# The forget gate's convolution of two recurrences by three VectorE taps on one projection, in place of four shifted TensorE products

## The chip, the cores and the metric

The kernel runs on one core of a Trainium2 chip. A core has TensorE (PE, matmuls; PEld is its weight load), VectorE (DVE), ScalarE (ACT), GpSimd (POOL) and SyncE (SP, which only issues transfers here). The metric is the device time of one execution in microseconds (us), lower is better. A profiled execution has a span, which the profile's rows divide, and a slightly longer time that counts what lies around it.

## The reference

The input x holds 4 sequences of 512 tokens with 128 channels, fp32. One block of a model is computed, each part on a layer norm of x and added to x:

1. a power attention with 16 heads of 8 channels and learned decay,
2. a mixture of experts: 8 experts, the best 2 for each token, hidden width 352,
3. a gated linear recurrence (HGRN),
4. the mixture of experts again.

The edited part is the third:

```python
i_raw = causal_depthwise_conv(x @ Wi, conv_i)      # 4 taps along time, per channel
f_raw = causal_depthwise_conv(x @ Wf, conv_f)
g_raw = x @ Wg
f = sigmoid(f_raw)
i = silu(i_raw) * (1 - f)
h_t = f_t * h_{t-1} + i_t                          # scan over the 512 tokens
o = h * rsqrt(mean(h*h) + eps) * g_norm_weight * silu(g_raw)
out = o @ Wo
```

A causal depthwise convolution with 4 taps is `sum over k of xp[:, k:k+T] * w[:, k]`, with 3 zeros ahead of the sequence.

## The kernel before

A planner (class Plan, lines 46 to 198) orders all work. Each piece of work is an `op` with an estimated cost on each engine that may do it, a priority, the tiles it reads and writes, and tiles it holds. The planner takes one op after the other, picks the engine and the order by these estimates, and gives out tiles from pools as they come free: "k2", 16 tiles of 128 x 512; "pad", 4 tiles with 3 zero columns ahead; "b1", single banks of PSUM. The instructions are issued on each engine in that order, so another cost or another engine for one op can move everything planned after it. Where the planner sees a gap on TensorE it puts filler matmuls (line 195).

Sequences are worked in two halves, q = 0 (sequences 0 and 1) and q = 1 (sequences 2 and 3); gen = 1 is the first mixture of experts and gen = 2 the second; stage (gen, q) is one of them for one half. The order is: attention for all, and for each stage

- `route(gen, q, i)` (line 865), for sequence i of the half: layer norm (lines 548 to 562) and transposition (L570), scores on TensorE (L875), the two best experts on VectorE (L899 to L920, exponential on ACT at L901), the token's scaled copies xk (L941 on ACT or L943 on VectorE), ranks by a small product (L927, L929), places (L952 to L998: i = 1 needs those of i = 0; L985 is the first that reads the ranks), and 8 scatters by GpSimd (L1004) that put rows of xk into the table xg; an i = 1 also computes `of` (to L1030), the offsets of the experts' weights for each block of 128 rows.
- `experts(gen, q)` (line 1042): 20 blocks. SP reads the expert's offset from `of` (L1089) and loads the block xb from xg (L1056) and the weights (L1099). TensorE transposes (L1068) and multiplies (L1106, L1126), ACT and VectorE do the gate (L1119, L1122), one of them copies the result (L1132), and GpSimd scatters it into the table yg (L1139).
- `combine` (line 1150): SP loads two tiles from yg for each sequence (L1158), VectorE (or GpSimd at the end) adds them to x (L1167).
- after gen 1, `hgrn` (line 1174) for each sequence, in priority beside the rest of the experts' work of the other half.

So a recurrence's result goes through the layer norm to the router of stage (2, q), whose VectorE work sets GpSimd's scatters and SP's loads.

In `hgrn(b)`, `xnT` is the normalized sequence with the channels on partitions, and hw holds Wi, Wf, Wg, Wo. The steps are

- L1180: `pi`, one product Wi by xnT (two passes on the chip for fp32).
- L1183: `pf`, four products of `wfk[k]` (Wf scaled by tap k, built once, L526 to L538) with xnT shifted by k, added up in one bank of PSUM.
- L1186: `pg`, one product with Wg.
- L1189 and L1193: the convolution of i: `acc = pi * tap 3` by ACT or VectorE, then three VectorE taps that read `pi` from PSUM shifted by one, two and three tokens and add into `acc`.
- L1196: `ft = tanh(0.5 * pf)` on ACT; L1198: silu of `acc`; L1202 and L1203: gate and input; L1205: the scan on VectorE; L1207, L1209, L1210: silu of `pg`, squares, gated output.
- L1215 and L1219: mean square by a product with ones, and the product with Wo; L1223 and L1225: the inverse root, the power on GpSimd; L1228: VectorE adds the result to x.

Of the kernel before, what the change touches and what calls it, by code (L numbers as in the profile page):

```python
# [11 lines left out]
AF = mybir.ActivationFunctionType  # L12
ALU = mybir.AluOpType
# [32 lines left out]
class Plan:  # L46
# [14 lines left out]
    def op(self, engs, fn, r=(), w=(), pri=0.0, late=None, after=(), hold=(), size=0.0,  # L61
           table=None):
        vals = list(hold)
        for v in hold:
            v.users += 1
        o = Op(dict(engs), fn, vals, pri, late, size, table)
        o.preds.update(after)
        for how, items in ((0, r), (1, w)):
            for it in items:
                v, part = it if isinstance(it, tuple) else (it, None)  # L70
                if v not in vals:
                    vals.append(v)
                    v.users += 1
                hit = v.parts if part is None else [p for p in (part, None) if p in v.parts]
                for p in hit:
                    o.preds.update(v.parts[p][0])
                    if how:
                        o.preds.update(v.parts[p][1])
        for how, items in ((0, r), (1, w)):
            for it in items:  # L80
                v, part = it if isinstance(it, tuple) else (it, None)
                if how:
                    if part is None:
                        v.parts = {}
                    v.parts[part] = ([o], [])
                else:
                    if part is None and v.parts:
                        for p in v.parts:
                            v.parts[p][1].append(o)
                    else:  # L90
                        v.parts.setdefault(part, ([], []))[1].append(o)
        o.preds.discard(o)
        self.ops.append(o)
        return o
# [147 lines left out]
def block_pass(  # L242
# [20 lines left out]
    nc = tc.nc  # L263
    B, T, C = x.shape
# [6 lines left out]
    CK = conv_i.shape[1]  # L271
    PAD = CK - 1
# [58 lines left out]
    op = plan.op  # L331

    def fixed(shape, nm, dt=FP):
        return Val(None, tile_of(shape, nm, dt))

    def new(kind):
        return Val(kind)

    def ve(n, ps=False):
        return 0.12 + n * (0.00098 if ps else 0.0009)  # L340

    def act(n):
        return 0.215 + n * 0.00071
# [4 lines left out]
    def either(n):  # L348
        return {"DVE": ve(n, True), "ACT": act(n)}
# [4 lines left out]
    def pe(n, passes=2):  # L354
        return passes * (0.03 + n * 0.0008)
# [17 lines left out]
    wfk = fixed([P, CK, C], "wfk")  # L373
# [4 lines left out]
    hw = fixed([P, 4, C], "hw")  # L378
    cw = fixed([P, 2, CK], "cw")
# [11 lines left out]
    slots_v = [Val(None, t) for t in vt + ot + gst + padt + xkt]  # L391
# [6 lines left out]
    def sp(fn, r=(), w=(), pri=0.0, late=2.2, after=(), cost=0.5, size=0.1, q="SP"):  # L398
# [4 lines left out]
       w=[xs[0]], pri=PRE, size=1.3)  # L403
# [4 lines left out]
    for b in range(1, B):  # L408
        sp(lambda e, b=b: e.dma_start(out=xs[b].t, in_=x[b].rearrange("(n p) c -> p n c", p=P)),
           w=[xs[b]], pri=PRE + 2 + b, size=1.3)  # L410

    def pl(fn, r=(), w=(), pri=PRE, n=128):
# [12 lines left out]
       r=[upto], w=[negm], pri=INIT)  # L425
# [5 lines left out]
       r=[ident], w=[hsel], pri=INIT)  # L431
# [12 lines left out]
    for k, t in enumerate(wst):  # L444
# [3 lines left out]
       r=[upto, ident], w=[upto_b], pri=-600.0)  # L448
# [22 lines left out]
    for k in range(14):  # L471
# [6 lines left out]
       r=[wnat, ident], w=[pw], pri=PRE)  # L478
# [695 lines left out]
    def hgrn(b, pri):  # L1174
        xn, xnT = new("k2"), new("pad")
        normed(b, xn, 0, pri)
        turned(xn, 0, xnT, PAD, pri)
        pf, pi, pg = new("b1"), new("b1"), new("b1")
        acc, ft, fg, sg, u, o, o2 = (new("k2") for _ in range(7))
        op({"PE": pe(T)}, lambda e: e.matmul(pi.t, hw.t[:, 0, :], xnT.t[:, PAD:], start=True, stop=True),  # L1180
           r=[(hw, 0), xnT], w=[pi], pri=pri, hold=[acc])
        op({"PE": CK * pe(T)}, lambda e: [
            e.matmul(pf.t, wfk.t[:, k, :], xnT.t[:, k : k + T], start=(k == 0), stop=(k == CK - 1))  # L1183
            for k in range(CK)
        ], r=[wfk, xnT] + slots_v[6:10], w=[pf], pri=pri, hold=[ft])
        op({"PE": pe(T)}, lambda e: e.matmul(pg.t, hw.t[:, 2, :], xnT.t[:, PAD:], start=True, stop=True),  # L1186
           r=[(hw, 2), xnT], w=[pg], pri=pri, hold=[sg])
        op(either(T), lambda e: (
# [2 lines left out]
           r=[pi, cw], w=[acc], pri=pri)  # L1191
        for k in range(PAD - 1, -1, -1):
            op({"DVE": 0.75}, lambda e, k=k: e.scalar_tensor_tensor(  # L1193
                acc.t[:, PAD - k : T], pi.t[:, 0 : T - PAD + k], cw.t[:, 0, k : k + 1], acc.t[:, PAD - k : T],
                ALU.mult, ALU.add), r=[pi, cw, acc], w=[acc], pri=pri)
        op({"ACT": act(T)}, lambda e: e.activation(ft.t, pf.t, AF.Tanh, scale=0.5),  # L1196
           r=[pf], w=[ft], pri=pri, table=("silu", "exp"))
        silus.append(op({"ACT": act(T)}, lambda e: e.activation(u.t, acc.t, AF.Silu),  # L1198
                        r=[acc], w=[u], pri=pri, table=("silu",)))
        op({"ACT": act(T), "DVE": ve(T)}, lambda e: (  # L1200
# [5 lines left out]
           r=[fg, u], w=[o], pri=pri)  # L1206
        silus.append(op({"ACT": act(T)}, lambda e: e.activation(sg.t, pg.t, AF.Silu),  # L1207
                        r=[pg], w=[sg], pri=pri + 1, table=("silu",)))
# [18 lines left out]
        for n in range(NB):  # L1227
# [3 lines left out]
               w=[(xs[b], None) if n == 0 else (xs[b], ("n", n))], pri=pri)  # L1231
# [4 lines left out]
    with tc.manual_schedule():  # L1236
# [15 lines left out]
        for gen in (1, 2):  # L1252
            for q in range(2):
                experts(gen, q, 100.0 * (2 * gen + q))
                for i in range(2):
                    combine(gen, q, i, CH[q] + i, gen == 2)
                    if gen == 1:
                        hgrn(seqs(q)[i], CH[q] + i)
                        route(2, q, i, CH[q] + (1.0 if i == 0 else 5.0))
# [4 lines left out]
        if over is not None:  # L1264
            op({"DVE": 0.2}, lambda e: e.tensor_scalar(over[1], over[0], float(NS), None, ALU.is_gt),
               r=[over_v], w=[over_v], pri=1000.0)
# [45 lines left out]
```

## Time and profile before

| | us |
|---|---|
| median of 3 runs | 535.82 (533.52 to 535.88) |
| profiled execution | 532.88 |
| span of the profiled execution | 530.7 |
| TensorE busy in it | 444.4 (84%) |
| VectorE busy | 301.3 (57%) |
| ScalarE busy | 300.8 (57%) |
| GpSimd busy | 249.1 (47%) |

The profiled execution lies 2.18 us over its own span and 2.9 us below the median. Its page has the busy time of each engine, the span cut in 40 slices of 13.3 us with the busy tenth of each engine and TensorE's granted clock, the chain of work that ended last, and the costliest groups of instructions. In a chain, "issue" is time in which an engine waited for nothing that the profile shows. In the list of waits a line names the waiting group and what released it, the total, the number of times and the longest.

The four recurrences run at 301 to 320 us (sequences 0 and 1, beside the last blocks of stage (1,1)) and at 393 to 415 us (sequences 2 and 3, beside the blocks of stage (2,0)).

### The profile page before, as it was taken

The page shows a single profiled execution, that of the slowest core. Times are in us where ns is not written, and L with a number is a line of the kernel's source. Part 1 is how long each engine was busy: PE and PEld are TensorE (multiplying, and loading weights), DVE is VectorE, ACT ScalarE, POOL GpSimd, SP SyncE. Part 2 cuts the span into 40 slices and gives each one's busy share as a digit, 9 for nine tenths or more (in the row PEclk, how much of TensorE's full clock was granted, in tenths as well). Part 3 has the DMA queues.
Part 4 walks back from the last instruction along what each step waited for, and adds up shares of the span by engine and source line. Part 5 has one row for each costly group of instructions (what it writes and reads, how often), then busy time and mean ns, then how long its engine had stood idle before and what let it go on. Part 6 is the DMA issues. An engine that isn't in the chain of part 4 may idle for free.

```text
span 530.7 us, 12313 instructions
## 1 busy us (share of the span) xinstructions
PE 444.4 (84%) x4319; PEld 346.7 (65%) x4319; DVE 301.3 (57%) x893; ACT 300.8 (57%) x512; POOL 249.1 (47%) x414
## 2 busy tenths in 40 slices
PE   8898999799869996999679999655999967689970
PEld 7554455355536562789579779645977957589960
DVE  7878598459848884675312776820177764013212
ACT  4689998599949994866124455601254643024420
POOL 6344154425362436334755536485063664816540
PEclk9999999699989997899979999857999987879995
DMA  3025100293083011226348814135582423639604
GB/s 94 12 58 143 47 1 17 73 187 50 5 229 95 1 30 40 61 82 182 109 133 265 256 35 131 55 86 150 152 252 56 124 81 98 178 110 312 201 21 124
DMA packets 67943, 57.55 MB, mean 108 GB/s; under 512 B 8576, under 2 KB 65822, under 8 KB 67872
## 3 DMA queue, kind: packets, MB, share of 16 engines
q1 hardware_dynamic: 60096, 46.65, 33.2%
q0 software_dynamic: 4608, 8.44, 4.7%
q10 hardware_dynamic: 3168, 1.57, 1.0%
q8 instruction: 37, 0.61, 0.5%
q14 instruction: 34, 0.28, 0.2%
HBM read 41.68 MB, written 16.00 MB: 109 GB/s over the span
## 4 chain that ended last, share of the span: by engine, by line
PE 53%; DVE 15%; issue 12%; ACT 10%; POOL 3%; DMA 2%; SPq 1%; another core or an unknown queue 1%; POOLq 0%; DVEq 0%; ACTq 0%
PE ps L1106 15%; PE ps L1126 9%; PE ps L719 6%; ACT k L735 4%; POOL yg L1139 3%; PE ps L777 3%; PE ps L1183 3%; PE ps L195 2%; ACT k L730 2%; ACT dec L703 2%; PE ps L773 2%; PE ps L1068 2%; PE ps L694 1%; PE ps L875 1%
## 5 line engine op out<-in xcount | busy, mean ns | idle before, releaser
L1106 PE MATMUL ps<-k,ws 128*128 128x128 f32 x960 | 125.6, 285 | 14.2 <-issue 13.5
L1106 PEld LDWEIGHTS ps<-k,ws 128*128 128x128 f32 x960 | 118.7, 200 | 17.9 <-issue 16.6
L1139 POOL DMA_INDIRECT yg<-y,xb x80 | 80.6, 1008 | 94.3 <-ACT y L1132 64.0
L1122 DVE TENSOR_TENSOR k<-k,ps 128x384 f32<-128x384 f32 x80 | 42.1, 548 | 114.4 <-PE ps L1106 59.8
L735 ACT ACTIVATE k<-k,aeps 128x1024 f32<-128x1024 f32 (+1 forms) x96 | 92.8, 1019 | 3.1 <-DVE k L731 2.8
L1126 PE MATMUL ps<-we,k 128*128 (+1 forms) x480 | 71.6, 296 | 14.8 <-issue 7.8
L1004 POOL DMA_INDIRECT xg<-xk,slt x64 | 62.8, 981 | 37.5 <-DVE slt L998 14.8
L1126 PEld LDWEIGHTS ps<-we,k 128*128 128x128 f32 (+1 forms) x480 | 64.1, 207 | 17.9 <-issue 9.0
L719 PE MATMUL ps<-k,k 32*128 32x384 f32 (+3 forms) x512 | 61.5, 498 | 8.0 <-issue 4.0
L1119 ACT ACTIVATE k<-ps 128x384 f32<-128x384 f32 x77 | 36.6, 489 | 51.5 <-PE ps L1106 32.9
L1132 ACT ACTIVATE y<-ps 128x128 f32<-128x128 f32 x72 | 19.7, 276 | 75.2 <-PE ps L1126 33.2
L751 POOL TENSOR_TENSOR k<-k,dec 128x256 f32<-128x256 f32 x29 | 22.2, 767 | 68.7 <-ACT k L735 45.1
L730 ACT ACTIVATE k<-ps 128x1024 f32<-128x1024 f32 (+1 forms) x49 | 45.8, 959 | 12.4 <-PE ps L719 5.5
L731 DVE TENSOR_SCALAR k<-ps 128x1024 int32<-128x1024 int32 (+1 forms) x47 | 44.2, 953 | 10.8 <-PE ps L719 8.2
L719 PEld LDWEIGHTS ps<-k,k 32*128 32x128 f32 x512 | 30.5, 198 | 24.2 <-issue 9.2
L195 PE MATMUL ps<-ones 128*128 128x128 f32 x232 | 37.1, 302 | 7.7 <-issue 7.7
L777 PE MATMUL ps<-k,vo 128*18 128x128 f32 x768 | 38.6, 280 | 5.0 <-ACT k L735 4.6
L362 ACT COPY k<-ps 128x512 f32<-128x512 f32 (+1 forms) x43 | 24.1, 571 | 29.2 <-PE ps L1068 18.3
L195 PEld LDWEIGHTS ps<-ones 128*128 128x128 f32 x232 | 32.2, 210 | 11.7 <-issue 9.7
L746 POOL TENSOR_TENSOR k<-k,dec 128x256 f32<-128x256 f32 x31 | 24.8, 812 | 27.7 <-ACT k L735 25.9
L703 ACT ACTIVATE dec<-ps 128x1024 f32<-128x1024 f32 x32 | 32.9, 1032 | 6.2 <-PE ps L719 3.7
L777 PEld LDWEIGHTS ps<-k,vo 128*18 128x18 f32 x768 | 21.2, 98 | 20.1 <-ACT k L735 14.6
(193 smaller groups left out, 625.4 us busy)
## 6 DMA issues: line engine op xcount, KB each, us to landing
ws<-in_L_ffn_w_dram SPq DMA_DIRECT2D x160, 176.0 KB
xb<-xg SPq DMA_DIRECT2D x20, 258.0 KB
xg<-zero SPq DMA_DIRECT2D x8, 451.5 KB
k<-yg SPq DMA_DIRECT2D x12, 256.0 KB
xg<-zero SPq DMA_DIRECT2D x4, 387.0 KB
yg<-y,xb POOLq DMA_INDIRECT x80
x<-in_L_attn_a_x_dram SPq DMA_DIRECT2D x4, 256.0 KB
we<-in_L_ffn_w_dram SPq DMA_DIRECT2D x8, 128.0 KB
```

Of the source, the lines that this page charges most:

```text
L195: self.nc.tensor.matmul(self.pairs[i][2][:, h, 0 : self.idle.shape[1]], self.idle, self.idle, start=True, stop=True)
L703: exps.append(op({"ACT": act(2 * T)}, lambda e: e.activation(dec[half].t, pd.t.rearrange("p k t -> p (k t)"), AF.Exp), r=[pd], w=[dec[half ...
L719: e.matmul(sps[hh // 2].t[:, hh % 2, c : c + tn * P], kT.t[r, s * P : (s + 1) * P], qT.t[r, t0 * P : (t0 + tn) * P], start=True, stop=True)
L730: e.activation(view(), sps[pr].t[:, :, 0:n], AF.Abs)
L731: if e is nc.scalar else e.tensor_scalar(view().bitcast(I32), sps[pr].t[:, :, 0:n].bitcast(I32), 0x7FFFFFFF, None, ALU.bitwise_and)
L735: op({"ACT": act(2 * n)}, lambda e, pa=pa: e.activation(pa.t, pa.t, AF.Square, bias=aeps.t), r=[pa, aeps], w=[(pa, "o"), (pa, "d")], pri=p ...
L777: e.matmul(oo.t[rows, (i - 1) * P : i * P], s, p, start=(ev == 0 and (i, j) == (1, 0)), stop=(ev == 1 and j == i - 1), skip_group_check=True)
L1004: d = e.indirect_dma_start(out=xgv.t, out_offset=bass.IndirectOffsetOnAxis(ap=slot.t[:, k * NB + n : k * NB + n + 1], axis=0), in_=xk[k].t ...
L1106: e.matmul(ph.t[:, w, kk * P : (kk + 1) * P], ws.t[:, w * HID + kk * P : w * HID + (kk + 1) * P], xT.t[:, k * P : (k + 1) * P], start=True ...
L1122: op({"DVE": ve(HD, True) + 0.03}, lambda e, ph=ph, sl=sl, hT=hT: e.tensor_tensor(hT.t[:, 0:HD], sl.t[:, 0:HD], ph.t[:, 1, 0:HD], ALU.mult ...
L1126: e.matmul(hp.t[:, 0:C], hT.t[0:fn, kk * P : (kk + 1) * P], wf[0:fn, bass.ds(regs[j] + kk * NE * C, C)], start=(kk == 0), stop=(kk == NF_ ...
L1139: d = e.indirect_dma_start(out=ygv.t, out_offset=bass.IndirectOffsetOnAxis(ap=xb.t[:, k, C : C + 1].bitcast(I32), axis=0), in_=y.t, in_off ...
```

## The change

For the sequences of the first half (`b < B // 2`) the forget gate's projection is one product with the unscaled Wf, and the convolution is done afterwards: tap 3 by a scaling out of PSUM (ACT or VectorE) into a new "k2" tile `cf`, taps 2, 1 and 0 by three VectorE instructions that read `pf` from PSUM, as it is done for `pi`. The tanh reads `cf` in place of `pf`. For the second half `cf` is `pf` and nothing differs. The scaled weights `wfk` are still built, since the second half uses them. The changed op also names Wf, (hw, 1), among what it reads. In the changed file the lines below the edit stand 13 further on.

```diff
-        op({"PE": CK * pe(T)}, lambda e: [
-            e.matmul(pf.t, wfk.t[:, k, :], xnT.t[:, k : k + T], start=(k == 0), stop=(k == CK - 1))
-            for k in range(CK)
-        ], r=[wfk, xnT] + slots_v[6:10], w=[pf], pri=pri, hold=[ft])
+
+        beside = b < B // 2
+        cf = new("k2") if beside else pf
+        op({"PE": (1 if beside else CK) * pe(T)}, lambda e: [
+            e.matmul(pf.t, wfk.t[:, k, :] if not beside else hw.t[:, 1, :], xnT.t[:, k : k + T],
+                     start=(k == 0 or beside), stop=(k == CK - 1))
+            for k in range(PAD if beside else 0, CK)
+        ], r=[wfk, (hw, 1), xnT] + slots_v[6:10], w=[pf], pri=pri, hold=[ft] + [cf] * beside)
+        if beside:
+            op(either(T), lambda e: (
+                e.activation(cf.t, pf.t, AF.Copy, scale=cw.t[:, 1, PAD:CK]) if e is nc.scalar else
+                e.tensor_scalar(cf.t, pf.t, cw.t[:, 1, PAD:CK], None, ALU.mult)),
+               r=[pf, cw], w=[cf], pri=pri)
+            for k in range(PAD - 1, -1, -1):
+                op({"DVE": 0.75}, lambda e, k=k: e.scalar_tensor_tensor(
+                    cf.t[:, PAD - k : T], pf.t[:, 0 : T - PAD + k], cw.t[:, 1, k : k + 1], cf.t[:, PAD - k : T],
+                    ALU.mult, ALU.add), r=[pf, cw, cf], w=[cf], pri=pri)
...
-        op({"ACT": act(T)}, lambda e: e.activation(ft.t, pf.t, AF.Tanh, scale=0.5),
-           r=[pf], w=[ft], pri=pri, table=("silu", "exp"))
+        op({"ACT": act(T)}, lambda e: e.activation(ft.t, cf.t, AF.Tanh, scale=0.5),
+           r=[cf], w=[ft], pri=pri, table=("silu", "exp"))
```

## Prediction

> **What bounds the kernel now.** I read the busy line first, then the slices, the chain that ended last, and the stretch from 300 to 420 us in windows, because the edited lines run there for the first two recurrences.
>
> ```profile
> PE 444.4 (84%) x4319; PEld 346.7 (65%) x4319; DVE 301.3 (57%) x893; ACT 300.8 (57%) x512; POOL 249.1 (47%) x414
> ...
> PE   8898999799869996999679999655999967689970
> ...
> PEclk9999999699989997899979999857999987879995
> ```
>
> TensorE (PE) leads, but not evenly: in slices 26 to 28 (332 to 371 us, 13.3 us each) its row falls to 6, 5, 5 and the granted clock to 0.8, 0.5, 0.7.
>
> ```profile
> 300.00:320.00 20.00, 19.84 (x109) 13.73 (x108) 14.68 (x35) 9.76 (x20) 7.57 (x9) 1.00 0.27 76
> 320.00:340.00 20.00, 18.02 (x163) 17.74 (x163) 15.06 (x73) 14.72 (x29) 10.75 (x19) 1.00 0.32 92
> 340.00:360.00 20.00, 9.43 (x51) 8.71 (x51) 7.31 (x33) 1.83 (x6) 17.11 (x32) 0.66 0.28 80
> 360.00:380.00 20.00, 15.20 (x107) 14.40 (x108) 1.09 (x3) 2.83 (x8) 5.42 (x10) 0.83 0.48 135
> ```
>
> (Busy us of PE, weight load, VectorE (DVE), ScalarE (ACT) and GpSimd (POOL), then the clock.) The edited products run where PE is full, 300 to 320; the hole they must shorten is at 346 to 377. The chain of work says the same:
>
> ```profile
> 302.25 3.43 PE ps L1183 x8
> ...
> 309.21 3.43 PE ps L1183 x8
> ...
> 312.64 0.89 PE ps L1219 x8
> ...
> 346.17 5.75 issue
> 351.92 4.75 PE ps L1106 x24
> ...
> 374.34 2.83 DMA xb<-xg
> ```
>
> Both four-product groups are on the chain, 3.43 us each. What feeds the hole is told by the waits of SP, ACT and POOL there:
>
> ```profile
> SPq L1089 <- DVE of L1030: 16.2, 1, 16.2
> ...
> ACT k L1119 <- remote: 12.5, 1, 12.5
> ...
> POOL xg L1004 <- DVE slt L998: 6.2, 1, 6.2
> ```
>
> SP reads expert numbers (L1089) and loads the blocks xb of stage (2,0) only after VectorE has finished the offsets (L1030, at 347.5); POOL starts its 16 scatters L1004 only when VectorE has the slots (L998, 336.9). So from 302 to 347 a chain leads from recurrence to normalization to router, mostly of VectorE latency. Then comes something I can see but not explain: from 348.4 to 364.2 all queues but POOL step about one instruction per 0.70 us (SP's register moves take 0.02 to 0.04 elsewhere), so ACT idles 12.5 us. It goes with unbroken runs of POOL's indirect transfers: 337.4 to 361.2 here, and 427.1 to 438.4 in the second half, where L985 waits 6.51 us.
>
> **The change part by part.** What moves I take from the two kernels' orders of instructions on each engine. Only the recurrences of sequences 0 and 1 change (302 to 320 us).
>
> Removed: three of four products. L1183 has 8 matmul passes per recurrence in 3.43 us of chain, 0.43 a pass; 6 passes go: 2.57 us, for two recurrences 5.15 us of PE.
>
> Added: one scaling from PSUM, like L1189 (0.678 us, on ACT in the new order), and three taps like L1193 (0.748 us; three dependent ones took 303.01 to 305.33, 2.32). Together 1.36 us of ACT and 4.6 us of VectorE. VectorE is 14.7 of 20 us busy here, so room exists, but the taps stand on the recurrence's own path: tanh (L1196) waited for the fourth product until 305.95; now it waits for the sixth tap.
>
> First recurrence: in the new order both conv's taps alternate. Six taps from 303.0 at about 0.77 end near 307.5 (305.33 before); tanh ends near 308.1 (306.54), the scan near 310.4 (308.85), the gated output L1210 near 311.25 (309.70): 1.55 us later. But its Wo product L1219 started only at 312.48, behind the second recurrence's L1183 (309.04 to 312.48) on PE. That queue is 5.15 us shorter, so L1219 starts at about 311.5, the ones-product L1215 ends near 313.1 (314.2) and x is updated at 316.1 (317.8): 1.6 us earlier, not 5.15. VectorE is what is late next.
>
> Router of sequence 0: L875 (326.05) comes 2.1 us earlier, L904 (330.18) 3.2; then three of L562 and two of L1122 are newly ahead of it on VectorE, and L998 ends 2.05 earlier. In POOL's new order one scatter of stage (1,1), L1139, moved from behind the 16 L1004 to before them, at 1.26 us pitch (337.35 to 338.62 for one): the scatters start about 1.5 us earlier, near 335.9.
>
> Second recurrence and router of sequence 1: the same taps, tanh 1.5 us later against its products, PE earlier by 5.15 less what waits for VectorE; offsets L1030 about 1.1 us earlier (346.4).
>
> Moved besides: on SP the four combine loads L1158 now stand ahead of a pair of weight loads L1099; SP waited 16.2 us right after, so they cost nothing unless that wait ends 4 × 0.7 us earlier. The seven L1089 stay seven (0.47 each). In the last stage one more addition L1167 stands on POOL instead of VectorE; it belongs to the last 17 us, where loads of 2.66 and 6.41 us bound it: between −0.3 and +1.0 us, taken as 0. The pool of 16 tiles holds one more for each of the two recurrences; the new order shows no engine's work displaced by it beyond what I listed: 0, and at most one tap chain, 2.3 us, if a normalization waits for a tile.
>
> From 347 on: the slow stretch is bounded by nothing on show. If it follows POOL's run, it shifts with it: −1.5 us. Then SP's loads and PE's (2,0) blocks start 1.1 to 1.5 us sooner, and the second half (PE full 380 to 420, all four products kept) is the same work.
>
> Sum: profiled execution 532.88 (span 530.7 and 2.18 around it) − 1.5 = 531.4. That execution lies 2.9 us under the median of the runs, 535.82, so in the median's terms 534.3.
>
> A rule that speaks against the change: the Trainium skill, VectorE: DVE Perf Modes, section Rules for kernel authors, advises accepting the slow rate for one operation on a matmul output, but copying it to SBUF if many follow. Here the rows are 748 ns for a tap on PSUM and 683 to 692 for the like-shaped L1203 on SBUF: three taps would gain 0.2 us and the extra copy costs 0.68, so by the row the rule would not pay and the sum keeps the PSUM taps; by the rule, 0.4 us for the two recurrences would be left lying, sum 531.0.
> Another, Perfetto Trace Analysis, section Identifying the Most-Contended Engine, says to optimize the engine of highest occupancy first; followed to the letter PE's 5.15 us would come off in full, 527.7. The waits above, on VectorE's L998 and L1030, make me take 1.5.
>
> **Rivals.**
> 1. Slower: the slow stretch falls on router work. One mechanism, place: POOL's run and the rank and place chain L985 to L1030 of sequence 1 (VectorE, 342 to 347.5). Before, this chain lay 5.8 to 10.2 us into the run and lost 0.7 us. With the scatter L1139 joined at the front, the run starts near 334.6, and the chain (1.1 earlier) lies 7.4 to 11.8 us into it. In the second half the slow stretch caught L985 about 8 us into its run and cost 6.51 us. The point from which it decides: L985 more than about 8 us after the run's first transfer. Price: up to 6.51 − 1.5 = +5.0: 537.9 profiled, 540.8 in the median. The run also holds six L1139 after the scatters, so the slowness may last to about 366 instead of 364.2. For it: the shifts just given. Against: 0.7 us of that chain was already inside without harm.
> 2. Faster: PE's 5.15 us comes through in full, because PE is on the chain from 299 to 334: 530.7. Or the blocks of (1,1) that now go ahead leave less in the slow stretch: SP alone needs 12.3 us after L1030, so the loads could begin near 359 instead of 374, at most −14 us. For it: in the new order all L1106 of (1,1) stand before the last rank product (before, two blocks, 351.9 to 356.7, did not). Against: VectorE's later tanh, and SP's slowness itself.
> 3. Nothing: PE's freed time fills with idle or filler matmuls (L195), the router leaves VectorE when it did: 535.8.
>
> **How the numbers follow.** About 0.5% (2.7 us) is what a measurement can tell from no change. Case A (−1.5, own range 532 to 537): 0.37. Rival 1, in full or in part (537 to 543): 0.34. Rival 2 (524 to 532): 0.25. Rival 3: 0.04. A is the likeliest: 534.3. Faster: rival 2 and 0.05 from A's low edge, 0.30. Same: A's middle, 0.28, and rival 3, 0.32. Slower: rival 1 and 0.04 from A's high edge, 0.38. Range: rival 1's whole price is 540.8, with the slow stretch's 1.8 us extra 542.6; rival 2's full PE gain 530.7, with about a third of the 14 us, 526. So 526 to 542 leaves about 0.2 out.
>
> **What will show it.** The edited product at 2 passes and 0.86 us; three taps at 0.75 and a 0.68 us scaling; tanh of the first recurrence released by VectorE near 307.5; x of sequence 0 at 316.1 instead of 317.8; L998 near 334.9 and the first L1004 near 335.9; SP's wait for the offsets ending near 346.4; first xb of (2,0) landing near 375.7 instead of 377.2; the end at 529.2 of span. It is wrong if ACT's "remote" idle moves from 12.5 us to over 16 or under 8, if L985 of sequence 1 waits several us, or if the second half's 6.51 us wait on L985 changes, which I priced at 0.

## The result and the profile after

| | before | changed |
|---|---|---|
| median, 8 runs each | 535.5 us (530.11 to 537.79) | 540.73 us (537.56 to 543.73) |
| ratio | 1 | 1.0103, 95% interval 1.0066 to 1.0139 |
| span of the profiled execution | 530.7 us | 536.6 us |

The changed kernel is 1.0% slower. A later measurement of the same two, beside three other kernels, gave 1.0152 (1.0094 to 1.0211). The forecast was 534.3 us, 1.5 less than before, which counted as no change; its largest single chance, 0.38, stood on slower. The measured time lies where the slower rival put it (540.8); whether for that rival's reason is taken up below.

The page of the changed kernel begins with this busy line:

```profile
PE 446.7 (83%) x4345; PEld 347.5 (65%) x4345; DVE 302.1 (56%) x897; ACT 303.6 (57%) x518; POOL 250.4 (47%) x415
```

TensorE has twelve passes of 512 columns less, and is busy 2 us longer all the same: the filler matmuls L195 rose from 232 to 270. The stretches around the edit (busy us of TensorE, weight load, VectorE, ScalarE and GpSimd, then the clock):

```profile
300.00:320.00 20.00, 19.09 (x135) 15.77 (x133) 17.64 (x45) 13.88 (x29) 8.27 (x14) 1.00 0.42 118
320.00:340.00 20.00, 17.14 (x155) 16.69 (x154) 16.79 (x73) 13.40 (x27) 12.04 (x17) 1.00 0.22 63
340.00:360.00 20.00, 11.44 (x88) 11.00 (x87) 7.49 (x37) 4.70 (x16) 11.73 (x23) 0.83 0.23 66
360.00:380.00 20.00, 11.42 (x67) 9.90 (x65) 0.00 (x0) 0.00 (x0) 10.20 (x20) 0.74 0.41 109
```

VectorE rose from 14.68 to 17.64 us in the first and from 15.06 to 16.79 in the second; in the last, VectorE and ScalarE did nothing at all for 20 us. What happened between is read from VectorE's timeline of the changed kernel (start, length, engine, line, operation; in brackets the idle time before it and what ended it):

```profile
304.34 1.53 DVE L1206 SCALAR_TENSOR_TENSOR k<-ps,cw,k 128x511 f32<-128x511 f32 x2 [0.80 <-ACT k L1202]
...
307.10 1.52 DVE L1196 SCALAR_TENSOR_TENSOR k<-ps,cw,k 128x510 f32<-128x510 f32 x2
...
310.44 1.23 DVE L1218 TENSOR_TENSOR_SCAN k<-k,k 128x512 f32<-128x512 f32 x1
311.70 0.75 DVE L1223 SCALAR_TENSOR_TENSOR k<-k,gn,k 128x512 f32<-128x512 f32 x1
312.37 0.74 DVE L1206 SCALAR_TENSOR_TENSOR k<-ps,cw,k 128x511 f32<-128x511 f32 x1
...
316.11 1.12 DVE L1241 SCALAR_TENSOR_TENSOR x<-ps,st,x 128x128 f32<-128x128 f32 x4
317.14 0.74 DVE L1196 SCALAR_TENSOR_TENSOR k<-ps,cw,k 128x509 f32<-128x509 f32 x1
...
319.54 1.19 DVE L1218 TENSOR_TENSOR_SCAN k<-k,k 128x512 f32<-128x512 f32 x1
```

The second recurrence's products are there at 310, but its taps begin at 312.37, because the first recurrence's taps and scan hold VectorE, and they end at 317.8, because x of sequence 0 (L1241) is in between. Its scan starts at 319.54. In the kernel before, the same instruction is

```profile
314.55 1.23 DVE L1205 TENSOR_TENSOR_SCAN k<-k,k 128x512 f32<-128x512 f32 x1
```

To leave out that this execution began its first recurrence 1.33 us later, I count from the first projection (301.1 and 302.5). The update of x of sequence 0 then starts at 13.7 us instead of 15.5, 1.9 earlier; that of sequence 1 at 23.5 instead of 19.3, 4.2 later; the scores of sequence 1's router (L875) at 34.2 instead of 27.6, 6.6 later.

In this pair of profiles the lateness goes no further. VectorE works through the router of sequence 0 first, and takes up the choice of experts for sequence 1 (L904 is its first step behind the exponential) at the same time as before, 36.5 us after the first projection in the kernel before and 36.6 in the changed one:

```profile
337.64 0.17 DVE L904 TENSOR_REDUCE sm<-sm 128x4 f32<-128x32 f32 x1
```

```profile
339.06 0.17 DVE L904 TENSOR_REDUCE sm<-sm 128x4 f32<-128x32 f32 x1
```

What is lost comes behind it.

The waits of the changed kernel from 330 to 390 us:

```profile
POOL xg L1004 <- issue: 9.2, 16, 6.4
ACT y L1132 <- remote: 9.1, 1, 9.1
DVE sm L985 <- PE ps L929: 7.4, 1, 7.4
```

and SP's own in that stretch:

```profile
SPq L1089 <- DVE k L1122: 25.3, 1, 25.3
```

Sequence 1's rank product (L929) was caught in the stretch in which ScalarE hardly steps: L985 waited 7.4 us, GpSimd's 16 scatters broke into 8 and 8 with a hole of 6.4, and SP got the offsets at 354.8 instead of 347.7. The first xb of stage (2,0) was issued at 378.4 instead of 374.3. A second profile of each showed the same: 382.0 after, 377.0 before, L985 waiting 7.5 us after and not at all before. There the choice of sequence 1 began later too, at 40.3 us against 36.6, and that of sequence 0 at 30.1 against 29.1; why is not shown. Counted from the first projection, the first xb of (2,0) was issued at 76.0 and 80.9 us in the changed kernel and at 73.2 and 74.9 before.

### The profile page after: what moved, and what is told of

The parts are those of the page before. It is cut to its first block, busy times and chain, and to the rows that moved or that the text cites. A ratio compares the mean times of both kernels' runs of the same rounds, so it can differ in the third digit from the quotient of the medians.

```text
span 536.6 us, 12357 instructions
## 1 busy us (share of the span) xinstructions
PE 446.7 (83%) x4345; PEld 347.5 (65%) x4345; DVE 302.1 (56%) x897; ACT 303.6 (57%) x518; POOL 250.4 (47%) x415
## 2 busy tenths in 40 slices
DMA packets 67943, 57.55 MB, mean 107 GB/s; under 512 B 8576, under 2 KB 65822, under 8 KB 67872
## 4 chain that ended last, share of the span: by engine, by line
PE 43%; DVE 18%; issue 12%; ACT 9%; POOL 7%; another core or an unknown queue 4%; DMA 3%; SPq 3%; POOLq 0%; DVEq 0%; ACTq 0%
PE ps L1106 11%; PE ps L1126 7%; PE ps L719 6%; POOL yg L1139 5%; PE ps L777 3%; ACT k L735 3%; PE ps L773 2%; ACT dec L703 2%; PE ps L1186 2%; PE ps L694 2%; SPq L1099 2%; ACT k L730 1%; DVE gst L466 1%; DVE k L1122 1%
## 5 line engine op out<-in xcount | busy, mean ns | idle before, releaser
L1106 PE MATMUL ps<-k,ws 128*128 128x128 f32 x960 | 123.6, 283 | 13.4 <-ACT y L1132 7.6
L1106 PEld LDWEIGHTS ps<-k,ws 128*128 128x128 f32 x960 | 115.9, 197 | 17.7 <-ACT y L1132 7.7
L1122 DVE TENSOR_TENSOR k<-k,ps 128x384 f32<-128x384 f32 x80 | 42.2, 549 | 116.3 <-PE ps L1106 81.2
L1126 PE MATMUL ps<-we,k 128*128 (+1 forms) x480 | 69.2, 291 | 7.6 <-DVE over L1022 2.9
L1126 PEld LDWEIGHTS ps<-we,k 128*128 128x128 f32 (+1 forms) x480 | 62.6, 203 | 10.8 <-issue 3.7
L719 PE MATMUL ps<-k,k 32*128 32x256 f32 (+3 forms) x512 | 62.5, 512 | 7.0 <-issue 4.0
L195 PE MATMUL ps<-ones 128*128 128x128 f32 x270 | 46.6, 314 | 21.9 <-issue 15.1
L195 PEld LDWEIGHTS ps<-ones 128*128 128x128 f32 x270 | 39.5, 219 | 28.4 <-issue 19.8
L362 ACT COPY k<-ps 128x512 f32<-128x512 f32 (+1 forms) x43 | 24.1, 570 | 47.8 <-PE ps L1068 36.6
L746 POOL TENSOR_TENSOR k<-k,dec 128x256 f32<-128x256 f32 x31 | 25.2, 825 | 27.9 <-ACT k L735 26.1
```

The lines of the kernel that those rows point to most:

```text
L195: self.nc.tensor.matmul(self.pairs[i][2][:, h, 0 : self.idle.shape[1]], self.idle, self.idle, start=True, stop=True)
L719: e.matmul(sps[hh // 2].t[:, hh % 2, c : c + tn * P], kT.t[r, s * P : (s + 1) * P], qT.t[r, t0 * P : (t0 + tn) * P], start=True, stop=True)
L1106: e.matmul(ph.t[:, w, kk * P : (kk + 1) * P], ws.t[:, w * HID + kk * P : w * HID + (kk + 1) * P], xT.t[:, k * P : (k + 1) * P], start=True ...
L1122: op({"DVE": ve(HD, True) + 0.03}, lambda e, ph=ph, sl=sl, hT=hT: e.tensor_tensor(hT.t[:, 0:HD], sl.t[:, 0:HD], ph.t[:, 1, 0:HD], ALU.mult ...
L1126: e.matmul(hp.t[:, 0:C], hT.t[0:fn, kk * P : (kk + 1) * P], wf[0:fn, bass.ds(regs[j] + kk * NE * C, C)], start=(kk == 0), stop=(kk == NF_ ...
```

## The experiments

All ratios are to runs of the kernel before made beside them. "x of sequence 0" and "x of sequence 1" are the starts of their updates and "first xb" is the issue of the first xb of stage (2,0), all in us from the first projection. The kernel before has 15.5, 19.3 and 73.2 or 74.9 in its two profiles, the changed one 13.7, 23.5 and 76.0 or 80.9.

| run | what | stretches | ratio (95%) | x of sequence 0 | x of sequence 1 | first xb |
|---|---|---|---|---|---|---|
| order_only | new order, four products, no taps | yes | 1.0163 (1.0136 to 1.0191) | 18.8 | 27.9 | 82.2 |
| oneprod | one product, no taps, own order | yes | 0.9999 (0.9972 to 1.0026) | 11.5 | 18.8 | 74.7 |
| first_only | taps for sequence 0 | yes | 0.9951 (0.9932 to 0.9970) | 14.8 | 18.6 | 75.9 |
| first_again | the same, later | yes | 1.0040 (1.0006 to 1.0074) | 14.8 | 18.6 | 74.8 |
| second_only | taps for sequence 1 | yes | 1.0006 (0.9983 to 1.0028) | 12.1 | 21.9 | 77.1 |
| work_only | old order, one product, taps | yes | 1.0114 (1.0077 to 1.0150) | 19.4 | 23.4 | 81.1 |
| hold_after | changed, scatters held back | yes | 1.0132 (1.0085 to 1.0179) | 13.7 | 23.5 | 73.8 |
| after_gap_2 | changed, scatters 3.4 us later | yes | 1.0144 (1.0100 to 1.0189) | 13.7 | 23.5 | 77.2 |
| before_late_2 | before, choice of sequence 1 later | yes | 1.0011 (0.9981 to 1.0041) | 15.5 | 19.3 | 72.1 |
| after_gap | changed, scatters 3.4 us later | no | 1.0018 (0.9987 to 1.0048) | 13.6 | 23.4 | 60.4 |
| before_gap | before, scatters 3.4 us later | no | 1.0050 (1.0021 to 1.0079) | 15.4 | 19.2 | 60.8 |
| before_late | before, choice of sequence 1 later | no | 1.0036 (1.0002 to 1.0069) | 15.4 | 19.2 | 60.9 |
| first_gap | taps for sequence 0, scatters later | no | 1.0052 (1.0018 to 1.0085) | 14.7 | 18.5 | 62.3 |
| taps_added | old order, four products, taps | no | 1.0112 (1.0074 to 1.0150) | 20.8 | 24.8 | 67.8 |
| prods_removed | old order, one product, no taps | no | 1.0010 (0.9980 to 1.0041) | 16.3 | 20.0 | 61.1 |

One thing must be known to read them. In the runs marked "no" the kernel before took 484 to 485 us, in all others 534 to 538, and in those six traces there is no stretch with steps of 0.70 us at all. Ratios are only taken within a group.

**First: order, products, or taps?**

order_only (new order of everything, work of before):

```diff
-            e.matmul(pf.t, wfk.t[:, k, :] if not beside else hw.t[:, 1, :], xnT.t[:, k : k + T],
-                     start=(k == 0 or beside), stop=(k == CK - 1))
-            for k in range(PAD if beside else 0, CK)
+            e.matmul(pf.t, wfk.t[:, k, :], xnT.t[:, k : k + T], start=(k == 0), stop=(k == CK - 1))
+            for k in range(CK)
...
-                op({"DVE": 0.75}, lambda e, k=k: e.scalar_tensor_tensor(
...
+                op({"DVE": 0.75}, lambda e: None, r=[pf, cw, cf], w=[cf], pri=pri)
```

> The planner is given the changed ops, so that every other instruction stands in the changed kernel's order, but the forget gate is still made by four products and the scaling and the taps emit nothing; the output is complete. Theory V (VectorE's taps of the second recurrence make the router of sequence 1 late, so that its rank product falls into the stall of GpSimd's first eight scatters): without taps the second recurrence's scan starts near 315.5 instead of 319.5, the wait of L985 is under 1 us, the 16 scatters form one run, and the time is 534 to 537. Rival O (the new order alone costs it, above all the scatter moved ahead of the 16): the wait of 7.4 us stays and the time is 540 to 543.

Measured: 545.72 us, 1.0163, L985 waits 7.6 us, the second scan at 323.3. Theory V's numbers failed here: without taps it was slower still. But this order was planned for a short TensorE queue, and the products push everything in it back (x of sequence 1 at 27.9 us), so the run does not tell what the order costs by itself.

oneprod:

```diff
+        k0 = PAD if b < B // 2 else 0
-        op({"PE": CK * pe(T)}, lambda e: [
+        op({"PE": (CK - k0) * pe(T)}, lambda e: [
...
-            for k in range(CK)
+            for k in range(k0, CK)
```

> One product with the scaled weights of tap 3, no taps on VectorE: the forget gate's three other taps are left out for sequences 0 and 1. It is the change's saving on TensorE without its cost on VectorE. Theory V: the scan of the second recurrence starts 3 to 5 us earlier than in the changed kernel, the wait of L985 is gone, and the time is 529 to 534. Rival P (TensorE's time does not matter here at all): 535 to 536.5. Rival O (order): anything from 535 to 541 with a wait of several us on L985 in spite of the early scan.

Measured: 537.87 against 537.01, 0.9999. Taking 5.15 us of work from the busiest engine, with nothing put in its place, bought nothing. The saving did reach the router: x of sequence 0 came at 11.5 us instead of 15.5 and its slots (L998) at 30.7 instead of 35.8. So GpSimd's run began at 332.4, sequence 1's rank product was caught (L985 waited 8.4 us), as the slower rival had it, and by the first xb (74.7) the gain was gone. With three taps left out the experts chosen can differ, but the transfers moved as much (57.54 MB, 57.55 before).

first_only and second_only (`beside = b == 0` and `beside = b == 1`):

> Only sequence 0 uses the taps, sequence 1 keeps the four products. Theory V: the second recurrence's scan is late by at most 1.5 us, the wait of L985 stays under 2 us, time 534 to 537. If half of the loss comes from each recurrence alone: 538.

> Only sequence 1 uses the taps. Theory V: six taps of the second recurrence on VectorE beside the first one's update of x; the scan of the second is late by 1 to 2.5 us; if this brings the rank product past the begin of the stall, L985 waits 5 to 8 us and the time is 538 to 541, otherwise 534 to 537. If half of the loss comes from each recurrence alone: 538.

Measured: 0.9951 and 1.0006, L985 waiting 8.3 us in the first and 3.2 in the second. Neither shows half of the loss, and a wait of 8 us on L985 comes without any loss here. When first_only was run again, it gave 1.0040, with the same 8.1 us on L985: its small gain does not repeat.

**Second: the exchanged work in the old order, and the wait taken away.**

work_only leaves the planner the costs of before, so each engine keeps its order, and issues one product and the taps in it (`scaled` and `tapped`, not shown, issue the scaling and the three taps):

```diff
+            if taps:
+                e.matmul(pf.t, hw.t[:, 1, :], xnT.t[:, PAD:], start=True, stop=True)
...
-            e.tensor_scalar(acc.t, pi.t, cw.t[:, 0, PAD:CK], None, ALU.mult)),
+            e.tensor_scalar(acc.t, pi.t, cw.t[:, 0, PAD:CK], None, ALU.mult), taps and scaled()),
...
-                ALU.mult, ALU.add), r=[pi, cw, acc], w=[acc], pri=pri)
+                ALU.mult, ALU.add), k == 0 and taps and tapped()), r=[pi, cw, acc], w=[acc], pri=pri)
```

> The counterpart of order_only: the planner is given the costs and ops of the kernel before, so that every engine's order is that of before, but for sequences 0 and 1 one product, the scaling (ACT, right behind that of i) and the three taps (VectorE, right behind those of i) are issued instead of four products; cf lies in two tiles of its own; the output is complete. Theory O (the new order costs it, the exchanged work itself saves): 531 to 534, both x updates of the first half as early as before or 1 to 2 us earlier. Theory V (VectorE's taps cost it in any order): 537 to 541, the second recurrence's scan 2 us later or more.

Measured: 543.67 against 537.85, 1.0114. Theory O fell: the work costs 1.1% in the old order too, and here no rank product was caught and the scatters formed one run. The two scans came 8.2 and 17.3 us after the first projection (6.5 and 13.4 before): 1.7 us late after one recurrence and 3.9 after two. But it is not the lateness of the changed kernel: here x of sequence 0 comes 3.9 us later than before (19.4) and its slots 6.4 later (42.2 against 35.8), while in the changed kernel both come earlier (13.7 and 34.3 in the first profile).

before_again and after_again, the second profiles told of above:

> The kernel before once more, for a second profile of it. If its first profile is typical, L985 of sequence 1 waits under 1 us, the 16 scatters of stage (2,0) form one run and its first xb is loaded near 374 us. If its orders lie on the edge of the stall (rank product at 341.2 us, stall from about 343), the second profile may show the wait of 7 to 8 us that all four variants so far show, and a time of 536 to 538.

> The changed kernel once more, for a second profile. The wait of L985 of 7 to 8 us and the first xb near 378 us are expected again, time 538 to 543; where it lies 2 to 5 us above the first profile, the stretch in which that is lost says what varies.

hold_after (no scatter of sequence 0 before sequence 1 has its slots):

```diff
+        if (gen, q) == (2, 0) and i == 1:
+            for held in puts:
+                held.preds.add(cast)
```

> The changed kernel, but GpSimd's eight scatters of sequence 0 in stage (2,0) wait until sequence 1 has its slots, so no run of scatters stands beside sequence 1's rank and place chain. Theory S (the stall comes with GpSimd's run of indirect transfers): L985 waits under 1 us, ACT has no idle of 9 us at 340 to 350, L998 of sequence 1 comes near 346, one run of 16 scatters follows and the stall falls beside it; the time is 537 to 543, since the scatters end no earlier. Rival (the stall has another cause and place, for instance TensorE's own waits): L985 waits 7 us all the same.

Measured: 544.14, 1.0132. L985's wait is gone and the stretch of slow steps moved with GpSimd's run to 353 to 374 us, as theory S said: it goes with the run. The time did not come back, although the first xb left at 376.9 (73.8 us after the first projection, no later than before); but the planner also changed the order behind it, and from there to the end it took 163.7 us instead of 156.4.

after_gap and its controls do it without a change of order:

```diff
+            if (gen, q, i, n, k) == (2, 0, 0, 0, 0):
+                e.tensor_copy(rest_[:, 0 : 2 * NB], slot.t)
+                for _ in range(6):
+                    e.memset(rest_, 0.0)
```

> The changed kernel in its own order, but GpSimd copies the slots and fills an unused tile six times (estimate 3.4 us, from the fills of 128x1296 at 1.2 us) between the slots of sequence 0 in stage (2,0) and the first of its scatters. That moves the begin of the run from 5.9 us before sequence 1's two best experts are known to about 2 us before. Theory S (the rank product of sequence 1 is caught by the stall of GpSimd's run when it is ready more than about 4 to 5 us after the run's begin, and this is a good part of the loss): L985 waits under 1 us, the 16 scatters form one run, the offsets come near 350 instead of 354.6 and 357.1, time 536.5 to 539, ratio 1.000 to 1.005. Theory V (VectorE's taps alone): L985's wait is gone but the time stays at 540 to 543.

> The same delay in the kernel before, as a control: the rank product is not caught there in the two profiles, so nothing is to be won; the scatters come 3.4 us later. Both theories: the ratio 1.000 to 1.007, no wait on L985.

> Taps for sequence 0 only, with the same delay ahead of its scatters as after_gap. Without the delay this kernel was 0.9951 of before, though L985 waited 8.3 us. Theory S: the wait goes, time 531 to 534, ratio 0.985 to 0.995. If the wait costs nothing by the end: 534 to 538, the delay alone costs up to 3.4.

before_late delays sequence 1's choice instead:

```diff
         dve(lambda e: (
+            (gen, q, i) == (2, 0, 1) and [e.tensor_copy(late_, xs[0].t.rearrange("p n c -> p (n c)")) for _ in range(5)],
```

> The kernel before, but VectorE copies an unused tile five times (estimate 2 us, by L1202's 0.43 for such a shape) right before sequence 1's choice of experts is complete in stage (2,0); nothing else is changed, no taps. The choice is then ready about 5.9 us after the run's begin instead of 3.8. Theory S: L985 waits 6 to 9 us, the 16 scatters break into two runs, and the time rises by more than the 2 us that were added: 539 to 543, ratio 1.006 to 1.013. Theory V: no wait, at most the 2 us: 1.000 to 1.004.

These four ran where before took 484.34 us, and no slow stretch was there to test: 1.0018 (0.9987 to 1.0048), 1.0050 (1.0021 to 1.0079), 1.0052 (1.0018 to 1.0085) and 1.0036 (1.0002 to 1.0069). The delay itself costs up to half a per cent there (before_gap). And after_gap, which holds the whole change with the delay on top, is at 1.0018: its median, 484.86 us, lies below the 487.33 of the kernel before with the same delay. Theory V, by which the taps alone make the loss, fails here. x of sequence 1 is 4.2 us late as ever (23.4 against 19.2), and the offsets come no later, 45.2 us after the first projection (278.17) in before_gap and 44.8 (278.43) in after_gap:

```profile
323.40 0.28 DVE L1035 TENSOR_SCALAR of<-sm 128x20 int32<-128x20 f32 x1
```

```profile
323.22 0.28 DVE L1035 TENSOR_SCALAR of<-sm 128x20 int32<-128x20 f32 x1
```

So without the slow stretches no loss of the change was seen in its own order; the changed kernel without the delay was not measured there, so this holds unless the delay wins something in it, which it does not in the kernel before. Two of the four were repeated beside the changed kernel itself.

> The changed kernel beside the next three on one chip. Where stretches with almost no steps on ScalarE and SyncE appear beside GpSimd's runs (before at 534 to 538): ratio 1.007 to 1.014, L985 waits 7 us. Where they do not (before at 484): theory S says 0.995 to 1.003, since the taps of the second recurrence then cost only the lateness of sequence 1's router, and theory V 1.006 to 1.014 as before.

> The changed kernel with 3.4 us between sequence 0's slots and its scatters. With the stretches: theory S 1.000 to 1.005 and no wait on L985; theory V 1.008 to 1.014. Without them: the same as the changed kernel or up to 0.005 more, as before_gap was 1.005.

> The kernel before with some 2 us of idle copies on VectorE ahead of sequence 1's choice. With the stretches: theory S 1.006 to 1.013, L985 waits 6 to 9 us; theory V 1.000 to 1.004. Without them: 1.000 to 1.005.

> Taps for sequence 0 only. With the stretches 0.993 to 0.997 again, although L985 waits. Without them 0.994 to 1.002: if its gain was TensorE's 2.6 us, it stays; if it was a stretch of the second half that it happened to miss, it goes.

Measured, with before at 534.59: the changed kernel 1.0152 (1.0094 to 1.0211), after_gap_2 1.0144, before_late_2 1.0011 (0.9981 to 1.0041). GpSimd's timeline of after_gap_2 shows the delay at its place, and L985 no longer waits:

```profile
338.30 0.21 POOL L1005 CAST rest__230<-slt 128x8 f32<-128x8 int32 x1
338.57 3.43 POOL L1007 MEMSET rest__230<- 128x512 f32 x6
...
342.23 0.99 POOL L1009 DMA_INDIRECT xg<-xk,slt  x1 [0.19 <-issue]
```

```profile
ACT y L1137 <- remote: 21.7, 1, 21.7
```

The 16 scatters are one run again and the offsets are made at 348.9 instead of 354.6, yet the first xb leaves at 378.6 and the time is the changed kernel's: ScalarE's idle time only moved and grew to 21.7 us. So taking the wait away by a delay wins nothing. It is no clean removal, since the delay holds GpSimd's run back as well: its last scatter starts 59.7 us after the first projection, 60.7 in the changed kernel and 55.2 before. That a wait of 8 us on L985 need not cost anything is shown better by oneprod, first_only and first_again. before_late_2 also refuted the bound that I had formed: the choice was ready 6.1 us after the run's begin, and its rank product ran at once.

**Third: a table in one order.** taps_added and prods_removed are the two missing corners beside before and work_only. Their cuts are against work_only.

taps_added (four products; scaling by one and taps of weight zero, on which the tanh waits):

```diff
-                e.matmul(pf.t, hw.t[:, 1, :], xnT.t[:, PAD:], start=True, stop=True)
+                for k in range(CK):
+                    e.matmul(pf.t, wfk.t[:, k, :], xnT.t[:, k : k + T], start=(k == 0), stop=(k == CK - 1))
...
-                    cf[:, PAD - k : T], pf.t[:, 0 : T - PAD + k], cw.t[:, 1, k : k + 1], cf[:, PAD - k : T],
+                    cf[:, PAD - k : T], pf.t[:, 0 : T - PAD + k], zero.t[:, 0:1], cf[:, PAD - k : T],
```

> The order of before, four products as before, and for sequences 0 and 1 the scaling (by one, on ACT) and three taps (with weight zero, on VectorE) that the tanh waits for; the output is complete. It has the change's added work without its saving. Theory V (the taps make the recurrences late, and that carries to the end): the second x update comes 5 us or more later after the first projection than in before (18.7 us), ratio 1.010 to 1.020. Rival P (time is set by TensorE's work): 1.000 to 1.005.

prods_removed (one product, tap 3 only, no scaling and no taps; the tanh reads pf):

```diff
-            if taps:
-                e.matmul(pf.t, hw.t[:, 1, :], xnT.t[:, PAD:], start=True, stop=True)
-            else:
-                for k in range(CK):
-                    e.matmul(pf.t, wfk.t[:, k, :], xnT.t[:, k : k + T], start=(k == 0), stop=(k == CK - 1))
+            for k in range(PAD if taps else 0, CK):
+                e.matmul(pf.t, wfk.t[:, k, :], xnT.t[:, k : k + T], start=(taps or k == 0), stop=(k == CK - 1))
...
```

> The order of before, one product with the scaled weights of tap 3 for sequences 0 and 1, no scaling and no taps: the forget gate's three other taps are left out there. It has the saving without the added work. Theory V, with the recurrence's path on VectorE and ACT: the second x update comes 2 to 5 us earlier, ratio 0.990 to 0.998. Rival P: the whole 5.15 us and more, 0.985 to 0.990. If the stall beside GpSimd's run takes it back, as oneprod has it: 0.998 to 1.003.

Measured, with before at 485.13: 1.0112 (1.0074 to 1.0150) and 1.0010 (0.9980 to 1.0041). In one order, the taps cost 1.1% with the products or without them (taps_added, work_only), and the products cost nothing measurable. taps_added and prods_removed ran where there is no slow stretch, work_only where there is one. Rival P fell in both. (The 18.7 us that the expectation of taps_added gives for the kernel before is an instruction that waits ahead of the update; the update itself starts at 19.3.)

Why the products are free in this order is in ScalarE's timeline of prods_removed, first recurrence:

```profile
281.22 0.63 ACT L1216 ACTIVATE k<-k 128x512 f32<-128x512 f32 x1 [1.68 <-DVE k L1211]
281.75 0.58 ACT L1214 ACTIVATE k<-ps 128x512 f32<-128x512 f32 x1
```

L1214 is the tanh of the forget gate. Its product was ready at 278.9, but it stands behind L1216, the silu of the convolved i, which waits for VectorE's taps of i. It starts 4.72 us after the first projection; in before_gap, with four products in the same order, 4.73 (282.90 − 278.17). x of sequence 1 starts at 20.0 us here and at 19.2 in before_gap. And TensorE's freed time turns into a wait, in its timeline of the same kernel:

```profile
277.89 1.02 PE L1191 MATMUL ps<-pd,wfk 128*128 128x512 f32 x2
281.27 1.26 PE L1204 MATMUL ps<-pd,hw 128*128 128x512 f32 x2 [2.36 <-DVE k L1211]
```

The next projection waits 2.36 us for VectorE's taps of i: nearly the 2.57 us that were taken out.

What the taps cost is in VectorE's timeline of taps_added:

```profile
279.93 2.32 DVE L1211 SCALAR_TENSOR_TENSOR k<-ps,cw,k 128x511 f32<-128x511 f32 x3 [0.35 <-ACT k L1207]
...
283.27 2.31 DVE L1199 SCALAR_TENSOR_TENSOR cf<-ps,zero,cf 128x511 f32<-128x511 f32 x3 [1.03 <-ACT cf L1195]
286.34 0.43 DVE L1220 TENSOR_SCALAR k<-k 128x512 f32<-128x512 f32 x1 [0.76 <-ACT k L1214]
```

The forget gate's taps are done after those of i on the same engine, and only then the tanh and the gate follow. In before, four products on TensorE and the three taps of i on VectorE ran side by side. So in the old order the taps stand in series on sequence 0's path: its x comes 5.4 us later than in before_gap (20.8 against 15.4), its slots 8.2 later (43.4 against 35.2), and the kernel takes 5.8 us more. In the changed kernel the two chains of taps alternate and x of sequence 0 comes earlier. So this explains the loss of work_only and taps_added, and not that of the changed kernel.

## Why the prediction was wrong, step by step

- **Removed, 2.57 us of TensorE per recurrence.** The size was right (the product is 0.86 us in the chain). That part of it comes through to the end is what failed. In the order of before, I took the L1183 groups of the chain of waits at their word, and the first tanh's start ("until 305.95") as the end of a wait for the products. Its row shows no idle time: ScalarE was at the silu of i, which VectorE's taps had released.

```profile
305.42 0.63 ACT L1198 ACTIVATE k<-k 128x512 f32<-128x512 f32 x1 [1.68 <-DVE k L1193]
305.95 0.58 ACT L1196 ACTIVATE k<-ps 128x512 f32<-128x512 f32 x1
```

In the second recurrence the tanh did wait for the products, until 312.68, but the taps of i ended at 312.44. Measured at the end: 0 (1.0010 in this order; 0.9999 in an order of its own, where some 5 us reached the slots of sequence 0 and were lost behind them).
- **First recurrence.** Right. With the 1.33 us by which this execution's first projection was later, I had written taps to 308.8, tanh to 309.4, scan to 311.7, x to 317.4; the rows have 308.6, 309.4, 311.7, 317.2.
- **Second recurrence and router of sequence 1: the failed step.** I predicted the offsets 1.1 us earlier. They came 5.8 us later (7.5 between the second profiles). Two things were wrong in it. I let "the same taps" start when their products were there; but VectorE had no idle time from 304.3 to 321.5 but two gaps of 0.29, the second recurrence's taps queued behind the first's chain and x, and x of sequence 1 came 4.2 us later, its scores 6.6. This took away the gain and, in the first pair of profiles, no more: the choice of sequence 1 began at 36.5 and 36.6 us. And the sum put the wait of L985 at nothing, leaving it to rival 1; it was 7.4 and 7.5 us.
- **From 347 on, "it shifts with it: −1.5".** The first xb of (2,0) was issued not 1.1 to 1.5 us earlier after the first projection but 2.8 and 6.0 later. From there to the end it took 156.4 and 156.6 us before, 158.2 and 157.6 after; that 1.4 us is within what executions differ by (before_late_2, the kernel before with a short delay, took 152.7). For the first pair: 1.33 us that lie ahead of the edit, 2.8 and 1.8 make the 5.9 us between the two spans.
- **A sign that I had named and priced at 0.** The second half's wait on L985 rose from 6.5 and 6.7 us to 8.6 and 8.7. Whether the end pays for it is not shown: oneprod has no such wait, and its second half took 159.3 us.
- **Router of sequence 0.** Only partly: L998 was to end 2.05 us earlier; the rows have 336.7 and 336.9, which against the first projection is 1.5 earlier, and in the second pair 2.2 later (38.0 against 35.8).
- **POOL's scatter moved ahead of the 16.** Right in place (336.71, then the scatters at 337.99), but the scatters came 0.7 us earlier against the first projection, not 1.5.
- **Rival 1, slower.** Its place and price were seen (L985 waited 7.4 us, up to 6.51 was written; 538.36 profiled, 537.9 was written). Its point of 8 us into the run did not hold: the choice of sequence 1 was ready some 6 us after the run's begin and was caught. As the whole cause it fell: oneprod, first_only and first_again have the same wait and lose nothing, after_gap_2 and hold_after lose as much without it. That the slow stretches, or whatever goes with them, have a part in it is what after_gap speaks for. The agreement of 540.8 with 540.73 is not a confirmation.
- **Rival 2, faster.** Fell with oneprod and prods_removed. The Trainium skill's rule in Perfetto Trace Analysis, section Identifying the Most-Contended Engine, followed to the letter, gave 527.7. By these runs 5.15 us less on the busiest engine was worth 0. The section after it, Optimization Strategy, asks what blocks that engine in its gaps; in the kernel before TensorE's waits from 295 to 380 us name mostly "issue" (7.2 and 5.7 us) and VectorE for 3.4, so this would not have pointed at the taps.

What stays open is why the changed kernel loses 1.0 to 1.5% where there are slow stretches. It is not the lateness of the second recurrence alone, since after_gap has it and loses nothing, and not the wait of L985 alone. Every trace of the changed order with stretches has GpSimd's last scatter of stage (2,0) start 4.5 us or more later after the first projection than before (59.7 or more, against 55.2); but second_only (60.3) and first_only (62.2) have that too, without a loss. No run separates these. For work_only and second_only, whose x of sequence 1 is late by 4.1 and 2.7 us with a loss of 1.1% and of nothing, the traces point to sequence 0, whose slots come 6.4 us later in the first and 2.8 earlier in the second; this was not tested by itself.

## What to carry to other kernels

Before moving work from the busiest engine to one with idle time, look at whether the two now run side by side on one dependency chain: moved work can then stand in series, as the taps did in the old order (1.1%), and the receiving engine's share of busy time does not tell. A group that stands on the chain of waits is worth only its lead over the next input of the same instruction, or of the instruction ahead in the queue; here that lead was at most a few tenths of a microsecond under a group of 3.43 us. When two copies of such a chain follow each other on one engine, count the second copy from the end of the first. And follow a lateness to the next engine that was busy anyway: 6.6 us on sequence 1's scores were nothing where VectorE took up its choice of experts. Last, a loss found in one order need not have the cause of an equal loss in another: the 1.1% of the taps in the old order came with and without slow stretches, the 1.0% of the change in its own order was not seen without them.

## What the runs showed that I had not expected

- The same kernel before took 534 to 538 us in some measurements and 484 to 485 us in others, on the same kind of chip and once on the same one. The difference goes with the stretches beside GpSimd's runs of indirect transfers in which SP steps once per 0.70 us: they are in every trace of the slower group and in none of the other. In the six traces without them the span from the offsets to the first xb of (2,0) is 13.4 to 16.8 us, with them 21.5 to 29.7. What sets them on or off was not found. In the old order the exchanged work costs the same in both (1.0114 and 1.0112); the changed kernel in its own order does not (1.0103 to 1.0152 with the stretches, 1.0018 without, there with the delay).
- Where they are, the stretch follows GpSimd's run: holding the scatters back moved it from 343 to 350 and 359 to 374 us to one of 353 to 374. A rank product ready 5 to 6 us after a run's begin was caught in some kernels for 7 to 8 us and not in before_late_2, so time since the run's begin is not the whole condition.
- Taps issued one after another on the same tile follow at 0.79 us ((2.32 − 0.748) / 2 in the kernel before); where those of i and of the forget gate alternate, in the changed kernel, they follow at 0.66 us (312.37, 313.03, 313.69), so two chains of taps cost less than twice one.
